# A two-layer graph kernel: biases spread by transposition, the last bank summed in PSUM in two pieces, and a load group moved one row tile later

## The chip, the core and the metric

The kernel runs on one core of a Trainium2 chip, in one launch. The metric is the device time in microseconds. Before the change its median is 930.77 us over three runs (930.59 to 931.49). The profile shown here is of one more execution of the same kernel, 930.15 us, whose instructions span 928.3 us.

## What is computed

There are 4096 nodes with 512 features each, a dense 4096 x 4096 adjacency matrix `adj`, and two layers, each with a residual. Cut to what matters:

```python
h = relu(layernorm(x))
# layer 0: attention within graphs of 128 nodes; the softmax is over the whole row
a = where(mask, (h @ Wq.T + bq) @ (h @ Wk.T + bk).T * scale, 0.0)
scores = (a + adj + adj) * where(mask, 1.0, -1e6)
x = x + (softmax(scores) * mask) @ (h @ Wv.T + bv)
# layer 1: graph attention with 8 heads of 64 features, over the edges adj > 0
h = relu(layernorm(x))
mx = einsum('nf,hfd->hnd', h, W)
logits = s_i[:, :, None] + t_j[:, None, :]
attn = softmax(where(adj > 0, logits, -inf))
x = x + concat_heads(attn @ mx)
```

In layer 1 the term `s_i` is the same for all neighbours of a row and cancels in the softmax. So a row's result is a masked sum of `exp(t_j) * mx_j` divided by the masked sum of `exp(t_j)`, and the aggregation is one product of the 0/1 mask with a table that holds both.

## The kernel before

**Tiling.** Rows go in 32 row tiles (`NT`) of 128 nodes. Features are four blocks of 128 (`KC`). TensorE multiplies a stationary operand of 128 columns, loaded anew for each matmul instruction, with a moving operand. A matmul of fp32 data is two instructions, one of float32r data is one, and a transposition of fp32 data is one.

**Start (`fold`, `spread_bias`).** The query and key weights are turned tile by tile (L205) and multiplied with each other (L242), so that layer 0 needs one product for its scores. The biases `bk` and `bq`, held with one feature to a partition, must be spread as rows over all partitions. For each block of 128 features, `spread_bias` multiplies a column broadcast to 128 x 128 with the identity (L187), and ScalarE copies the result to SBUF (L192). The same is done with the vector `u_col` (L231, copied at L235). ScalarE's order here is written by hand: the four copies of the key weights (L206), the two of the biases, the four of the query weights. TensorE's order here is the scheduler's.

**Layer 0.** It goes over pairs of row tiles, in an order written by hand for all engines. The adjacency matrix streams through SBUF once, 64 loads of 1 MB, and what layer 1 needs of it, a mask of one byte per edge, is written to DRAM. The queue of the sync engine (SP) issues these loads in program order, and each waits until its buffer is free and for what was issued ahead of it.

**Between the layers.** Layer 1's table is made for row tiles 8 to 31 by a loop over `i`. In step `i` the sync queue loads row `i + 12` (`load`, L775), VectorE and ScalarE normalise row `far = i + 10`, and VectorE turns it (`turn`). After each fourth row `store` writes the group of four to DRAM (L420), and `move` brings it back transposed as `hT4` (four loads, L428), which waits for that store to land. TensorE projects tile `i` (L271), ScalarE takes the exponential, VectorE multiplies (`weigh`, L280), and `split` makes the table `parts[i]` of two float32r parts, the rounded value and what is left of it[...]. When `far` is 33 the buffers of the rows are given up, and the mask words of the first row tile are loaded (`load_words`, L291).

**Layer 1's aggregation.** The table has 522 columns (512 of features, 8 of denominators, 2 spare), as `CB` = 3 banks of `CW1` = 174. A matmul of `product` (L322) takes one bank with both parts side by side, 348 columns, which lie side by side in PSUM:

```python
nc.tensor.matmul(
    pg[:, : 2 * CW1].rearrange("p (s w) -> p s w", s=2)[:, :, :n],
    at[:, j, :], part(j)[:, c, :, :n],
    start=(j == 0), stop=(j == NT - 1),
)
```

A row tile is 32 x 3 such matmuls. After them ScalarE copies the first part and VectorE adds the second. The last row tile goes bank by bank, in the order 2, 0, 1, so that most of its closing work lies beside matmuls. For each bank ScalarE copies the first part (L887), VectorE adds the second (L888), multiplies by the reciprocal of the denominators (`rb`, L905) and adds the row of layer 0 (L906), and the store is issued from ScalarE's queue (L907). Bank 2 comes first because it holds the denominators. A check of the fast path's conditions is folded into one number (`bad_i`, L900 to L903), and the branch on it at the end skips a general version.

Of the kernel before, what the change touches and what calls it, by code (L numbers as in the profile page):

```python
# [9 lines left out]
F32 = mybir.dt.float32  # L10
# [5 lines left out]
ALU = mybir.AluOpType  # L16
# [4 lines left out]
P = 128  # L21
N = 4096
D = 512
NT = N // P
# [5 lines left out]
BY = 4  # L30
# [6 lines left out]
CB = 3  # L37
CW1 = 174
# [6 lines left out]
AHEAD = 10  # L45
WARM = 10
LO = 8
# [6 lines left out]
def kernel(  # L54
# [22 lines left out]
    nc = tc.nc  # L77
# [13 lines left out]
    ident = const.tile([P, P], F32, name="ident")  # L91
# [82 lines left out]
    def fold(sb, tmp, work, ps_t, ps_p, loads, between):  # L174

        wkT_sb = load_weight(tmp, wkT, "wkT_sb", KC, tag="lo")
        nc.sync.dma_start(bk_sb, bk)
        nc.sync.dma_start(bq_sb, bq)  # L180
        wqT_sb = load_weight(tmp, wqT, "wqT_sb", KC, tag="lo")
        loads()

        def spread_bias(b):
            pp = ps_p.tile([P, D], F32, name="pp")
            for k in range(KC):
                nc.tensor.matmul(  # L187
                    pp[:, ts(k, P)], b[:, k : k + 1].to_broadcast([P, P]), ident,
                    start=True, stop=True,
                )  # L190
            row = work.tile([P, D], F32, name="b_row", tag="hn")
            nc.scalar.copy(row, pp)  # L192
            return row


        pt = ps_t.tile([P, KC, P], F32, name="pt")
        for _ in range(WARM):
            nc.tensor.transpose(pt[:, 0, :], ident, ident)
        nat = []
        for n, wT in enumerate((wkT_sb, wqT_sb)):  # L200
            w = tmp.tile([P, KC, D], F32, name=f"w{n}", tag="lo")
            for k in range(KC):
                pt = ps_t.tile([P, KC, P], F32, name="pt")
                for m in range(KC):
                    nc.tensor.transpose(pt[:, m, :], wT[:, k, ts(m, P)], ident)  # L205
                nc.scalar.copy(w[:, :, ts(k, P)], pt)  # L206
                if n == 0 and k == KC - 1:
                    rows = [spread_bias(b) for b in (bk_sb, bq_sb)]
            nat.append(w)
        wk, wq = nat  # L210
        m_sb = sb.tile([P, KC, D], F32, name="m_sb")
        c_sb = sb.tile([P, KC], F32, name="c_sb")
        u_col = sb.tile([P, KC], F32, name="u_col")
        u_sb = sb.tile([P, D], F32, name="u_sb")
        z_sb = sb.tile([P, 1], F32, name="z_sb")
        for dst, wT, row in ((u_col, wqT_sb, rows[0]), (c_sb, wkT_sb, rows[1])):
            for k in range(KC):
                wb = work.tile([P, D], BF16, name="wb", tag="hu", bufs=1)
                nc.vector.scalar_tensor_tensor(
                    wb, wT[:, k, :], SCALE, row, ALU.mult, ALU.mult, accum_out=dst[:, k : k + 1]  # L220
                )
        zk = sb.tile([P, KC], F32, name="zk")
        zp = sb.tile([P, 1], F32, name="zp")
        nc.vector.scalar_tensor_tensor(
            zk, bq_sb, SCALE, bk_sb, ALU.mult, ALU.mult, accum_out=zp
        )
        for m in range(KC):
            if m == 2:
                pp = ps_p.tile([P, D], F32, name="pp")
                for k in range(KC):  # L230
                    nc.tensor.matmul(  # L231
                        pp[:, ts(k, P)], u_col[:, k : k + 1].to_broadcast([P, P]), ident,
                        start=True, stop=True,
                    )
                nc.scalar.copy(u_sb, pp)  # L235
                pp = ps_p.tile([P, D], F32, name="pp")
                nc.tensor.matmul(pp[:, :1], zp.to_broadcast([P, P]), one, start=True, stop=True)
                nc.scalar.copy(z_sb, pp[:, :1])
            between(m, 0)
            pp = ps_p.tile([P, D], F32, name="pp")  # L240
            for k in range(KC):
                nc.tensor.matmul(  # L242
                    pp, wq[:, k, ts(m, P)], wk[:, k, :], start=(k == 0), stop=(k == KC - 1)
                )
            between(m, 1)
            nc.scalar.mul(m_sb[:, m, :], pp, SCALE)
        return m_sb, c_sb, u_sb, z_sb
# [138 lines left out]
    parts = []  # L386
    with ExitStack() as straight:
# [4 lines left out]
        with ExitStack() as prep:  # L392
# [71 lines left out]
            with (  # L464
# [160 lines left out]
                first = []  # L625
# [151 lines left out]
            with by_hand:  # L777
                ahead = LO + AHEAD + 5
                for i in range(LO + AHEAD, ahead):
                    load(i)  # L780
                move(LO // BY + 1)
                before = None
                low = lambda: None
                for i in range(LO, NT):
                    far = i + AHEAD
                    if far + 2 >= ahead:
                        load(far + 2)
                    if far % BY == 1 and LO + AHEAD < far <= NT + 1:
                        move(far // BY - 1)
                    if far == NT + 1:  # L790

                        begun.close()
                        sb3a = straight.enter_context(
                            tc.tile_pool(name="sb3a", bufs=1, reuse_waits="tile")
                        )
                        ata = sb3a.tile([P, NT, P], F32R, name="ata")
                        words = load_words(sb3a, 0)
                    if i == NT - 4:
                        at8 = turn_words(sb3a, words)
                    if i in (NT - 3, NT - 2):  # L800
                        half = (i - NT + 3) * NW // 2
                        widen(ata, at8, half, half + NW // 2)
                    low()
                    if far < NT:
                        of[far] = moments(rows[far])
                    if LO + AHEAD < far <= NT:
                        turn(far - 1, rows[far - 1], (keep, sb4)[(far - 1) // BY % 2])
                        if far % BY == 0:
                            store(far // BY - 1)
                    pm = project1(ps_p, hTs[i], w1x)  # L810
                    if before:
                        low = finish(*before, later=True)
                    if far < NT:
                        norm(rows[far], rows[far], of[far])
                    before = (weights(i, pm), pm, upper[i])
                    if far < NT:
                        nc.scalar.activation(rows[far], rows[far], AF.Relu)
                low()
                finish(*before)
# [55 lines left out]
        at = mask_of(i)  # L875
        ps_l = straight.enter_context(tc.tile_pool(name="ps_l3", bufs=2, space=PSUM))
        tot = sb3.tile([P, EW], F32, name="tot")
        rb = sb3.tile([P, EW], F32, name="tot")
        for c in (CB - 1, 0, 1):
            if c == 1:  # L880
                pg = ps_g.tile([P, CB, 512], F32, name="pg")[:, 0]
            else:
                pg = ps_l.tile([P, 512], F32, name="pl")
            for j in range(NT):
                product(pg, at, lambda j: parts[j], j, c, False)
            part = tot[:, ts(c, CW1)]
            nc.scalar.copy(part, pg[:, :CW1])  # L887
            nc.vector.tensor_tensor(part, part, pg[:, CW1 : 2 * CW1], ALU.add)  # L888
            if c == CB - 1:
                r = heads_rest(tot)  # L890
                nc.vector.tensor_scalar(held[:, 5:6], tot[:, ES : ES + 1], 0.0, None, ALU.is_gt)
                all_held = small.tile([P, 1], F32, name="all_held")
                nc.vector.tensor_reduce(all_held, held, AX.X, ALU.min)
                nc.vector.tensor_copy(
                    rb[:, :D].rearrange("p (h d) -> p h d", d=HD),
                    r[:, :, None].to_broadcast([P, H, HD]),
                )
            if c == 0:
                pt = ps_g.tile([P, CB, 512], F32, name="pg")[:, 0, :P]
                nc.tensor.transpose(pt[:1, :], all_held, ident)  # L900
                least = small.tile([1, 1], F32, name="least")
                nc.vector.tensor_reduce(least, pt[:1, :], AX.X, ALU.min)
                nc.vector.tensor_scalar(bad_i, least, 1.0, None, ALU.is_lt)  # L903
            here = slice(c * CW1, min((c + 1) * CW1, D))
            nc.vector.tensor_tensor(tot[:, here], tot[:, here], rb[:, here], ALU.mult)  # L905
            nc.vector.tensor_tensor(tot[:, here], tot[:, here], row[:, here], ALU.add)  # L906
            nc.scalar.dma_start(out[ts(i, P), here], tot[:, here])  # L907
    bad = nc.values_load(bad_i[0:1, 0:1], min_val=0, max_val=1)
# [294 lines left out]
```

## Time and profile before

| | |
|---|---|
| time, median of 3 | 930.77 us |
| span of the profiled execution | 928.3 us |
| TensorE's clock granted | 0.999 |
| aggregation, 31 row tiles (from the chain of waits) | 473.07 us, 2976 matmuls |
| its last row tile, banks 2 and 0 | 10.21 us, 64 matmuls |
| its last row tile, bank 1 | 5.16 us, 32 matmuls |
| two spread biases (L187) | 16 matmul instructions, 1.2 us and 1.2 us busy |
| spread `u_col` (L231) | 8 matmul instructions, 1.1 us busy |

The page gives each engine's busy time over the whole span. The chain of waits follows the end of the run back to what released each step. A line of a group names the line of the kernel, the engine, what is written from what, the shapes and the count, then busy time and the mean of one, then the idle time ahead of it and what ended that. PE stands for TensorE's matmuls and PEld for its weight loads, which can run beside them. DVE is VectorE, ACT is ScalarE, POOL is GpSimd, and SPq and ACTq are the queues of DMA issues.

### The profile page before, as it was taken

What the parts mean: (1) busy time and instruction counts of PE and PEld (TensorE: products, weight loads), DVE (VectorE), ACT (ScalarE), POOL (GpSimd) and SP (SyncE); (2) the same over time, 40 slices, a digit from 0 to 9 for tenths busy, and PEclk for the clock granted to TensorE, in tenths of its full rate; (3) what the DMA queues carried; (4) which work ended last, traced back from release to release, by engine and by line L of the source; (5) the groups of instructions that cost most, each with busy time, mean ns of one, the idle gap of its engine ahead of it and who ended that gap; (6) DMA issues with size and microseconds to landing.
All of it is one profiled execution on the core that took longest, in us unless ns stands there. A gap on an engine that the chain in (4) does not pass through costs nothing.

```text
span 928.3 us, 13021 instructions
## 1 busy us (share of the span) xinstructions
PE 919.4 (99%) x4933; PEld 803.4 (87%) x4933; DVE 474.3 (51%) x1016; ACT 261.1 (28%) x507; POOL 160.8 (17%) x344
## 2 busy tenths in 40 slices
PE   9999999999999999999999999999999999999997
PEld 6776676767767778889999999999999999999997
DVE  4577987677778776736272424232333323242412
ACT  5477667655566653321000000000000000000000
POOL 1112111132211225644010101010101010101010
PEclk9999999999999999999999999999999999999999
DMA  8999999999899766762212122222222131313111
GB/s 333 415 333 390 366 372 377 345 368 352 309 350 370 238 203 182 208 154 57 69 52 85 55 83 61 76 69 68 82 56 83 55 91 46 91 46 92 46 46 37
DMA packets 63941, 165.01 MB, mean 178 GB/s; under 512 B 7042, under 2 KB 23810, under 8 KB 54658
## 3 DMA queue, kind: packets, MB, share of 16 engines
q1 hardware_dynamic: 54370, 147.35, 47.4%
q10 hardware_dynamic: 9504, 16.78, 4.8%
q8 instruction: 40, 0.66, 0.3%
q14 instruction: 27, 0.22, 0.1%
HBM read 122.16 MB, written 41.94 MB: 177 GB/s over the span
## 4 chain that ended last, share of the span: by engine, by line
PE 90%; DMA 6%; DVE 1%; ACT 1%; POOL 1%; issue 0%; SPq 0%; DVEq 0%; ACTq 0%
PE pg L322 52%; PE pp L517 10%; PE pp L504 10%; PE pp L271 9%; PE pss L578 3%; PE pp L609 3%; DMA xg<-x 2%; PE pp L242 1%; DMA row<-x_d 1%; PE pt L135 1%; DMA x_d<-x 1%; PE pl L322 1%; DMA a<-adj 1%; DMA hT_d<-blocks 0%; DMA bk_sb<-bk 0%
## 5 line engine op out<-in xcount | busy, mean ns | idle before, releaser
L322 PE MATMUL pg<-part,ata 128*128 128x348 f32 (+1 forms) x1536 | 246.8, 321 | 0.0
L322 PEld LDWEIGHTS pg<-part,ata 128*128 128x128 f32 x1536 | 244.5, 188 | 0.1
L322 PE MATMUL pg<-part,atb 128*128 128x348 f32 x1472 | 236.8, 322 | 0.0
L322 PEld LDWEIGHTS pg<-part,atb 128*128 128x128 f32 x1472 | 234.6, 189 | 0.1
L336 ACT COPY tot<-pg 128x522 f32<-128x522 f32 x31 | 18.5, 597 | 454.0 <-PE pg L322 454.0
L547 ACT ACTIVATE junk<-a 128x2048 bf16<-128x2048 f32 (+15 forms) x92 | 124.5, 1353 | 1.3
L517 PE MATMUL pp<-wv,hT 128*128 128x512 f32 x256 | 114.9, 592 | 0.0
L308 DVE CAST atb<-at 128x4096 fp32r<-128x4096 fp8e4 x16 | 36.7, 2295 | 152.6 <-PE pg L322 152.6
L271 PE MATMUL pp<-w1x,hT 128*128 128x256 f32 (+1 forms) x512 | 114.1, 383 | 0.3 <-DVE e L280 0.3
L504 PE MATMUL pp<-hT,m_sb 128*128 128x256 f32 x512 | 113.2, 379 | 0.0
L271 PEld LDWEIGHTS pp<-w1x,hT 128*128 128x128 f32 x512 | 96.7, 190 | 16.2 <-issue 1.9
L308 DVE CAST ata<-at 128x4096 fp32r<-128x4096 fp8e4 (+1 forms) x17 | 36.9, 2168 | 140.5 <-PE pg L322 140.4
L504 PEld LDWEIGHTS pp<-hT,m_sb 128*128 128x128 f32 x512 | 96.2, 190 | 12.8 <-issue 0.5
L517 PEld LDWEIGHTS pp<-wv,hT 128*128 128x128 f32 x256 | 47.9, 190 | 54.3 <-issue 53.5
L144 DVE TENSOR_SCALAR a<-a 128x512 fp8e4<-128x512 f32 x256 | 90.4, 447 | 1.3 <-DMA a<-adj 1.3
L854 POOL COPY den_all<-tot 128x1 f32<-128x1 f32 x31 | 5.7, 184 | 365.9 <-DVE tot L337 365.9
L858 POOL TENSOR_TENSOR tot<-tot,row 128x512 f32<-128x512 f32 x31 | 39.9, 1287 | 61.9 <-DVE tot L342 59.9
L121 POOL TENSOR_SCALAR ve<-mv 128x1 f32<-128x1 f32 x64 | 15.1, 236 | 190.4 <-DVE mv L119 190.3
L255 POOL TENSOR_TENSOR part<-e,part 128x522 fp32r<-128x522 f32 x32 | 40.7, 1271 | 12.8 <-ACT part L252 12.8
L123 POOL TENSOR_TENSOR rstd<-ve,neghalf 128x1 f32<-128x1 f32 x64 | 41.1, 642 | 5.3
L299 DVE STREAM_TRANSPOSE at<-mw 128x1024 f32<-128x1024 f32 x32 | 39.6, 1237 | 0.0
L280 DVE TENSOR_TENSOR e<-pp,e 128x256 f32<-128x256 f32 x64 | 25.1, 411 | 27.0 <-PE pp L271 13.7
(114 smaller groups left out, 658.4 us busy)
## 6 DMA issues: line engine op xcount, KB each, us to landing
a<-adj SPq DMA_DIRECT2D x64, 1024.0 KB, 8.4
a_d<-a SPq DMA_DIRECT2D x32, 512.0 KB, 9.0
mw<-a_d SPq DMA_DIRECT2D x128, 128.0 KB, 3.9
row<-x_d SPq DMA_DIRECT2D x60, 256.0 KB, 3.7
xg<-x SPq DMA_DIRECT2D x16, 512.0 KB, 10.7
x_d<-x ACTq DMA_DIRECT2D x32, 256.0 KB, 7.3
hT_d<-blocks SPq DMA_DIRECT2D x8, 1024.0 KB, 4.8
hT<-hT_d SPq DMA_DIRECT2D x32, 256.0 KB, 6.2
```

The source lines that it names most:

```text
L123: nc.gpsimd.tensor_tensor(rstd, ve, neghalf, ALU.pow)
L144: nc.vector.tensor_scalar(a8v[:, u], av[:, u], 0.0, None, ALU.is_gt, saturate=False)
L255: nc.gpsimd.tensor_sub(dst[:, :, 1, :], e3, dst[:, :, 0, :].bitcast(F32))
L271: nc.tensor.matmul(pm[g][:, :n], hT[:, k, :], w1x[:, k, g * HW : g * HW + n], start=(k == 0), stop=(k == KC - 1),)
L299: nc.vector.transpose(at8.rearrange("p c n b -> p (c n b)").bitcast(F32).rearrange("p (c u n) -> p c u n", c=NW, n=B), mw.rearrange("p u ( ...
L308: nc.vector.tensor_copy(at[:, c0 * BY : c1 * BY].rearrange("p (c b) q -> p c b q", b=BY), at8[:, c0:c1].rearrange("p c q b -> p c b q"),)
L322: nc.tensor.matmul(pg[:, : 2 * CW1].rearrange("p (s w) -> p s w", s=2)[:, :, :n], at[:, j, :], part(j)[:, c, :, :n], start=(j == 0), stop= ...
L504: nc.tensor.matmul(pp[:, : G * P], m_sb[:, k, ts(m, P)], hT[:, k, :], start=(k == 0), stop=(k == KC - 1),)
L517: nc.tensor.matmul(pp, hT[:, k, ts(t, P)], wv[:, k, :], start=(k == 0), stop=(k == KC - 1))
L547: nc.scalar.activation(junk[:, c0:c1], a[:, c0:c1], AF.Exp, scale=2.0 * NEG, accum_out=sums[:, n : n + 1],)
L578: nc.tensor.matmul(pss[:, t, :], gT[:, k, ts(t, P)], hT[:, k, ts(t, P)], start=(k == 0), stop=(k == KC - 1),)
L858: nc.gpsimd.tensor_add(num, num, row)
```

## The change

There are three edits. The first spreads the two biases and `u_col` with transpositions of the broadcast column in place of matmuls with the identity. The second moves `move`, for the groups that it handles in the loop between the layers, from the step after the store to one step later, so that one more row load stands ahead of it in the sync queue. The third treats the last bank of the last row tile in two pieces of 88 and 86 columns. Both parts of each row tile are added up in the same PSUM columns by two matmuls, so that no copy and no addition is left after them, and the second piece alone is left to be closed at the end.

```diff
         def spread_bias(b):
             pp = ps_p.tile([P, D], F32, name="pp")
             for k in range(KC):
-                nc.tensor.matmul(
-                    pp[:, ts(k, P)], b[:, k : k + 1].to_broadcast([P, P]), ident,
-                    start=True, stop=True,
-                )
+                nc.tensor.transpose(pp[:, ts(k, P)], b[:, k : k + 1].to_broadcast([P, P]), ident)
...
-                    nc.tensor.matmul(
-                        pp[:, ts(k, P)], u_col[:, k : k + 1].to_broadcast([P, P]), ident,
-                        start=True, stop=True,
+                    nc.tensor.transpose(
+                        pp[:, ts(k, P)], u_col[:, k : k + 1].to_broadcast([P, P]), ident
                     )
...
-                    if far % BY == 1 and LO + AHEAD < far <= NT + 1:
+                    if far % BY == 2 and LO + AHEAD < far <= NT + 2:
                         move(far // BY - 1)
...
-        for c in (CB - 1, 0, 1):
+        CW2 = CW1 // 2 + 1
+        for c, c0, w in ((CB - 1, 0, CW1), (0, 0, CW1), (1, 0, CW2), (1, CW2, CW1 - CW2)):
+            first = c * CW1 + c0
+            here = slice(first, min(first + w, D))
             if c == 1:
-                pg = ps_g.tile([P, CB, 512], F32, name="pg")[:, 0]
+                pg = ps_g.tile([P, CB, 512], F32, name="pg")[:, 0, :w]
+                for j in range(NT):
+                    for part in range(2):
+                        nc.tensor.matmul(
+                            pg, at[:, j, :], parts[j][:, c, part, c0 : c0 + w],
+                            start=(j + part == 0), stop=(j == NT - 1 and part == 1),
+                        )
+                nc.vector.tensor_tensor(tot[:, here], pg, rb[:, here], ALU.mult)
             else:
                 pg = ps_l.tile([P, 512], F32, name="pl")
-            for j in range(NT):
-                product(pg, at, lambda j: parts[j], j, c, False)
-            part = tot[:, ts(c, CW1)]
-            nc.scalar.copy(part, pg[:, :CW1])
-            nc.vector.tensor_tensor(part, part, pg[:, CW1 : 2 * CW1], ALU.add)
+                for j in range(NT):
+                    product(pg, at, lambda j: parts[j], j, c, False)
+                part = tot[:, ts(c, CW1)]
+                nc.scalar.copy(part, pg[:, :CW1])
+                nc.vector.tensor_tensor(part, part, pg[:, CW1 : 2 * CW1], ALU.add)
...
-            here = slice(c * CW1, min((c + 1) * CW1, D))
-            nc.vector.tensor_tensor(tot[:, here], tot[:, here], rb[:, here], ALU.mult)
+            if c != 1:
+                nc.vector.tensor_tensor(tot[:, here], tot[:, here], rb[:, here], ALU.mult)
             nc.vector.tensor_tensor(tot[:, here], tot[:, here], row[:, here], ALU.add)
```

## The prediction, made before the changed kernel was run

> **What bounds the kernel now.** I read the page first, then TensorE's waits, the chain of waits, the weight loads by shape, and three stretches in order of time. On the page TensorE is busy for all but 9 us:
>
> ```profile
> PE 919.4 (99%) x4933; PEld 803.4 (87%) x4933; DVE 474.3 (51%) x1016; ACT 261.1 (28%) x507; POOL 160.8 (17%) x344
> ```
>
> There is one weight load (PEld) for each matmul instruction. The list of TensorE's waits (us in total, times, longest) shows how little there is to win in the middle:
>
> ```profile
> PE pp L609 <- DVE e L280: 0.8, 1, 0.8
> ...
> PE pp L271 <- DVE e L280: 0.3, 1, 0.3
> PE pt L205 <- ACT w L206: 0.2, 1, 0.2
> ```
>
> The rest of the 9 us lies before the first data and after the last matmul. So removed matmul time counts, a removed wait counts 0.3 us, and work that is added to TensorE is added to the end. The end of the chain of waits (start, us, what):
>
> ```profile
> 917.57 5.16 PE pg L322 x32
> 922.75 0.31 ACT tot L887
> 923.09 0.35 DVE tot L888
> 923.46 0.35 DVE tot L905
> 923.84 0.34 DVE tot L906
> ```
>
> The last bank takes 32 matmuls in 5.16 us, 0.161 us each for 348 columns, and then four small operations in a row from 922.75 to 924.18 before the last store is issued.
>
> What decides this case is how fast narrow matmuls can follow one another, so I look at weight loads by shape (count, busy us, mean ns of one):
>
> ```profile
> L322 PEld LDWEIGHTS pg<-part,atb 128*128 128x128 f32 x1472 | 234.6, 189 | 0.1
> ...
> L205 PEld LDWEIGHTS pt<-ident,wqT_sb 128*128 128x128 f32 x16 | 1.8, 141 | 0.4 <-ACT w L206 0.4
> ...
> L900 PEld LDWEIGHTS pg<-ident,all_held 128*1 128x1 f32 x1 | 0.1, 82 | 0.0
> ```
>
> A load of one column takes 82 ns, a full one in the aggregation 189: 107 ns for 127 more columns. The loads of transpositions take 141, so 59 more. Whether a load bounds the pace shows where matmuls are tiny, in order of time (start, us):
>
> ```profile
> 18.93 0.30 PEld L237 LDWEIGHTS pp<-one,zp 128*128 128x128 f32 x2
> 19.03 0.28 PE L237 MATMUL pp<-one,zp 128*128 128x1 f32 x2
> ...
> 19.15 0.30 PEld L242 LDWEIGHTS pp<-w,w 128*128 128x128 f32 x2
> ```
>
> Matmuls of one column each, yet the loads start at 18.93 and 19.15 with one between: **0.11 us a matmul, whatever its width.** At 348 columns the 0.161 us of streaming hides that; at 88 it can't.
>
> [...] Loads of L322 have the length of the FP32 ones (189 against 190 at L271)[...]
>
> **The change part by part.**
>
> *Last bank.* Removed: 32 matmuls, 5.16 us. Added: 2 pieces x 32 tiles x 2 parts = 128 matmuls of 88 or 86 columns. Each brings its own load, also where two in a row have the same weights: before, three in a row (one per bank) share `at[:, j]`, and the counts are still 4933 and 4933. By columns one would stream in 88 x 0.161/348 = 0.041 us; the load needs 0.11. No float32r matmul under 344 columns is in the trace, so I bound it. [...] Above: what a column costs in an ordinary fp32 matmul of 128 columns, two instructions of 0.112 (16 of L578 in 1.79 us), so 0.224/128 x 88 = 0.154. I take L237's 0.111: 128 x 0.111 = 14.2 us, +9.0; the last matmul drains some 0.1 sooner (322 ns for 348 columns, 169 for one, so about 210). Net **+8.9** (13.7 us and +8.4 below, 19.7 us and +14.4 above). Nothing else is on TensorE's queue behind it, and the end waits for it: all of it is on the path.
>
> *What follows the last matmul.* Before: 922.72 (end of the last matmul) to 924.21 (issue of the store), 1.49 us. After: one product out of PSUM and one addition, 86 columns each, [...] plus three hand-overs of 0.03: 0.60. **-0.9.** The first piece's product, addition and store lie beside the second piece's 7 us, and cost nothing. The second piece takes the other ps_g buffer, whose last reader (L902) is done by 917.9: no wait.
>
> *Biases by transposition.* An fp32 matmul is two instructions (x8 for four at L187), a transposition one (x16 for sixteen at L205). So 24 instructions of 0.111 become 12 of 0.109: 2.66 - 1.31 = 1.35 us off TensorE. Of the 0.9 from the two biases little arrives: L205's last four transpositions wait for ScalarE's copies already now (the 0.2 us above), and ScalarE's row of copies begins with the one at 8.67, whose four transpositions now follow 10 instructions (10 x 0.111) and then follow 8 (8 x 0.109), and 0.05 sooner by the quicker first load: 0.29 sooner. The 0.45 of u_col arrives in full, since u_col is ready at 16.3 and used at 18.1. Sum 0.74. But the next stage leans on the DMA, which is full (us, PE, PEld, DVE, ACT, POOL, clock, DMA share, GB/s):
>
> ```profile
> 40.00:60.00 20.00, 20.00 (x91) 14.14 (x90) 13.03 (x35) 12.53 (x25) 2.46 (x7) 1.00 0.89 335
> 60.00:80.00 20.00, 20.00 (x95) 14.30 (x94) 14.67 (x40) 13.35 (x26) 3.26 (x9) 1.00 1.02 390
> ```
>
> At 187 TensorE waits 0.8 us for `e`, whose VectorE sat behind an x load that landed late. If transfers alone set that moment, TensorE only waits 0.74 longer; the gap at 40 to 60 says buffers still have a word there, so part passes. **-0.5**, from 0 to -0.75.
>
> *The group moved later.* Between the layers the sync queue holds the hT loads of `move`, which wait for the store's landing, ahead of row loads. VectorE then waits for a row, and TensorE for VectorE:
>
> ```profile
> 386.40 0.69 DVE L117 BATCH_NORM_STATS2 stats<-row 128x6 f32<-128x512 f32 x1 [2.91 <-DMA row<-x_d]
> ...
> 388.36 45.83 PE L271 MATMUL pp<-w1x,hT 128*128 128x264 f32 x208 [0.29 <-DVE e L280]
> ```
>
> One more row load goes ahead of `move`: that row was issued at 380.30 and may now go at 374, landing before 383.5, where VectorE wanted it. hT is still loaded four tiles (14 us) ahead of use, against 6.2 us to land. **-0.3**, or 0 if the next row takes its place. The order now lets the mask words of row tile 1 be turned (1.23 us on VectorE) ahead of a product L280; its PSUM buffer is wanted over 3 us later, so nothing.
>
> Sum: +8.9 - 0.9 - 0.5 - 0.3 = **+7.2, 938.0 us.**
>
> **Rivals.**
> 1. *Narrow float32r matmuls stream no quicker than fp32* (0.154): +14.4 - 1.7 = +12.7, 943.5 us. For it: no narrow one is in the trace. Against: 344 and 348 columns run at about a quarter of fp32's cost per column (0.46 against 1.75 ns).
> 2. *The second load of the same weights is free, or loads go as quickly as those of transpositions* (59 ns): 7.0 to 7.6 us, about +2 - 0.1 - 1.7, 931 us, no change. Against: 189 against 141 ns, and equal counts.
> 3. *Loads don't bound at all*: 128 x 0.041 = 5.2 us, no loss, and with all 1.35 of the biases -0.9 - 0.3 - 1.35 = -2.5, 928.3 us, **faster**. Against: L237's 0.11.
>
> **How the numbers follow.** Forecast 0.62, rival 1 0.26, rival 2 0.07, rival 3 0.05. The forecast spans 937.2 (+8.4 - 0.9 - 0.35 - 0.75) to 939.0 (0.1125 a matmul, +9.1 - 0.9, no gain elsewhere); rival 1 spans 942.8 (0.150) to 945.2 (0.160). The range 936.8 to 945.0 holds both, 0.87. Slower 0.88, within 0.2% (1.9 us) 0.07, faster 0.05.
>
> **What would show it.** The chain's last TensorE piece grows from 5.16 to about 14.2 us, with 0.11 between matmuls; 0.15 is rival 1, 0.06 rival 2, 0.04 rival 3. From the last matmul's end to the store's issue: 0.6 us. L271 without a wait on L280. The wait before L609 at 187: 0.8 us if the biases' gain passes, up to 1.5 if the DMA keeps it. Wrong would be a time under 936, which needs narrow matmuls quicker than their loads.

## The result, and the profile after

The changed kernel takes **945.92 us** (median of six runs, 945.04 to 948.83) against 930.62 (929.95 to 931.49) before: 1.0168 times the time, with an interval of 1.0153 to 1.0183. The forecast of slower was right, but the size was not: +15.3 us against +7.2, just outside the range of 936.8 to 945.0. Line numbers from here on are those of the changed kernel, whose matmuls of `product` stand at L318 and whose new narrow ones at L884.

The end of its chain of waits (start, us, what):

```profile
904.88 10.21 PE pl L318 x64
915.09 0.11 PE pg L907
915.20 23.55 PE pg L884 x128
...
938.78 0.26 DVE tot L888
...
939.06 0.25 DVE tot L913
```

The span grew by 15.0 us (928.3 to 943.3), and the two chains say where. The last row tile is reached at 904.88 instead of 907.26, -2.38. The last bank takes 23.55 us instead of 5.16, +18.39. What follows it takes 4.55 us (938.75 to 943.3) instead of 5.57 (922.73 to 928.3), -1.02. The sum is +14.99, so the whole loss lies in the last bank, and it is more than the other two edits and the shorter close give back.

23.55 us over 128 matmuls is 0.184 us each, above every price in the prediction. But a mean hides what happened. The narrow matmuls alone, in three stretches (us, PE busy, PEld busy, TensorE's clock, DMA share, GB/s; a count in brackets includes instructions that lie across an edge of the stretch):

```profile
915.20:918.90 3.70, 3.70 (x36) 3.70 (x35) 1.00 0.12 31
918.95:922.00 3.05, 3.05 (x17) 3.05 (x16) 0.52 0.02 5
922.00:938.70 16.70, 16.70 (x79) 16.58 (x78) 0.50 0.01 4
```

For 3.7 us they come at 0.11 us each, as forecast. **Then the clock column falls to 0.50**, and the same instructions come at 0.213. The groups of their weight loads say it too, in the first stretch and in a later one (count, busy us, mean ns of one, idle before):

```profile
L884 PEld LDWEIGHTS pg<-part,atb 128*128 128x128 f32 x35 | 4.0, 192 | 0.0
...
L884 PEld LDWEIGHTS pg<-part,atb 128*128 128x128 f32 x89 | 19.1, 333 | 0.0
```

On the page the engine looks as busy as ever; only the clock's row shows a change, in its last digit:

```profile
PE   8999999999999999999999999999999999999998
...
PEclk9999999999999999999999999999999999999995
```

PE's 9 means that instructions followed one another without a pause. It doesn't say that the array was at work: 88 columns are streamed in some 0.041 us, an estimate from the wide matmuls (88/348 of 0.161), while the matmuls come 0.111 us apart and weight loads are busy for all of it (3.70 of 3.70 us). In the trace's record of the clock the fall is at 919.07, and the record stays at 0.50 for the 26.2 us that are left of it. The first narrow matmul starts at 914.96, 4.1 us earlier (the chain counts it from 915.20, when the work ahead of it has drained). Such times after the first narrow matmul are counted from its own start from here on.

### The profile page after: what moved, and what is told of

Same layout as the page of the kernel before. It is cut to its first block, busy times and chain, and to the rows that moved or that the text cites. A ratio compares the mean times of both kernels' runs of the same rounds, so it can differ in the third digit from the quotient of the medians.

```text
span 943.3 us, 13191 instructions
## 1 busy us (share of the span) xinstructions
PE 935.5 (99%) x5017; PEld 820.0 (87%) x5017; DVE 475.2 (50%) x1017; ACT 261.1 (28%) x506; POOL 162.3 (17%) x344
## 4 chain that ended last, share of the span: by engine, by line
PE 99%; DMA 0%; ACT 0%; SPq 0%; DVE 0%; issue 0%
PE pg L318 50%; PE pp L267 12%; PE pp L500 12%; PE pp L513 12%; PE pss L574 3%; PE pp L605 3%; PE pg L884 2%; PE pt L135 1%; PE pp L238 1%; PE pl L318 1%; DMA bk_sb<-bk 0%; PE pss L597 0%; SPq L152 0%; PE pt L202 0%; PE pp L187 0%; ACT w L203 0%
## 5 line engine op out<-in xcount | busy, mean ns | idle before, releaser
L318 PE MATMUL pg<-part,ata 128*128 128x348 f32 (+1 forms) x1536 | 246.8, 321 | 0.0
L318 PEld LDWEIGHTS pg<-part,ata 128*128 128x128 f32 x1536 | 244.4, 188 | 0.1
L318 PE MATMUL pg<-part,atb 128*128 128x348 f32 (+1 forms) x1440 | 231.5, 321 | 0.0
L318 PEld LDWEIGHTS pg<-part,atb 128*128 128x128 f32 x1440 | 229.5, 188 | 0.0
```

The lines of the kernel that those rows point to most:

```text
L318: nc.tensor.matmul(pg[:, : 2 * CW1].rearrange("p (s w) -> p s w", s=2)[:, :, :n], at[:, j, :], part(j)[:, c, :, :n], start=(j == 0), stop= ...
```

## The experiments

**The theory,** which the runs below are to test: TensorE's clock is lowered when the array streams too little over a stretch of a few microseconds (4.1 in the changed kernel), even if its queue never pauses. Matmuls of 88 columns, held to 0.111 us by their weight loads, stream too little, by the estimate above 0.37 of the time. **Rivals:** narrow float32r matmuls are slow in themselves (the prediction's rival 1); the clock falls because the run is ending; weight loads without a pause lower the clock, whatever is streamed.

What the expectations call a window of 3.4 us is a step in the records of the clock: it is full for 914.77 us in the changed kernel and in e4 (the last bank's edit alone), 918.19 in e1 (the other two edits) and 921.60 before, which is 268, 269 and 270 times 3.413 (in e1 and before, the fall comes after the last matmul).

### The parts of the change, one at a time

Three kernels take one or two of the three edits, with the rest as before. The fourth is the last bank's edit alone. e1 has the first two:

```diff
-                nc.tensor.matmul(
-                    pp[:, ts(k, P)], b[:, k : k + 1].to_broadcast([P, P]), ident,
-                    start=True, stop=True,
-                )
+                nc.tensor.transpose(pp[:, ts(k, P)], b[:, k : k + 1].to_broadcast([P, P]), ident)
...
-                    if far % BY == 1 and LO + AHEAD < far <= NT + 1:
+                    if far % BY == 2 and LO + AHEAD < far <= NT + 2:
```

e2 has the first hunk (with that of `u_col`), e3 the second, and e4 only the hunk of the last bank.

> Biases by transposition and the group moved later, last bank as before. The changed kernel's trace reached the last row tile's bank 2 at 904.88 us instead of 907.26, 2.4 us sooner, so the closing bank alone is the loss. This theory expects 930.6 - 2.4 = 928.2 us. Rival: part of the 2.4 us is chance of the transfers in one execution (the 1.0 us at 187); then 929.2 us. If the loss were spread elsewhere than in the last bank, it would stay above 931 us.

> Biases by transposition alone. Theory: TensorE reaches layer 0 0.65 us sooner, and the loads behind it follow, so the wait at 187 us disappears too (1.0 us): 930.6 - 1.7 = 928.9 us. Rival (as the prediction had it): the full DMA keeps the gain, the wait at 187 grows from 0.8 to 1.5 us, and the time is 930.3 us or more.

> The group moved later alone. Theory: both hitches of the loop between the layers go (0.14 us at 373, 0.53 us at 388, start to start): 930.6 - 0.67 = 929.95 us, and the wait at 187 stays. Rival: the wait at 187 is gone here too, so it was not the biases' doing: 928.9 us.

> The last bank in two pieces alone. Clock theory: matmuls of 88 columns follow at 0.111 us, TensorE's clock halves about 4 us after they begin, from then on 0.213: 36 x 0.111 + 92 x 0.213 = 23.6 us for 128, against 5.2, and 1.0 us less after it: 930.6 + 18.4 - 1.0 = 948 us, with a scatter of up to 3 us from where the halving falls. Rival, narrow matmuls are slow in themselves: the same pace from the first to the last, 0.18 each, and no scatter. Rival, the loads alone: 938.7 us.

| kernel | median us (runs) | ratio to before, interval |
|---|---|---|
| before | 930.98 (47) | |
| e1, biases and group | 929.40 (18) | 0.9985, 0.9978 to 0.9993 |
| e2, biases | 929.45 (22) | 0.9980, 0.9971 to 0.9989 |
| e3, group | 930.38 (14) | 0.9992, 0.9984 to 1.0001 |
| e4, last bank | 947.84 (5) | 1.0175, 1.0158 to 1.0193 |

The last bank's edit alone costs what the clock theory said (948), a little more than the whole change. The halving is in its trace as well, at 921.95, 3.5 us after the first narrow matmul there, and its last bank takes 24.13 us:

```profile
918.72 24.13 PE pg L888 x128
```

The scatter (946.07 to 949.0) fits too, but proves little, as the kernel before scatters as widely in many runs. By the medians the parts add up: +16.9 with the last bank alone and -1.6 with the other two edits make the +15.3 of the whole.

The other two edits together gain 1.4 us by their interval's middle (0.7 to 2.0). So the forecast of 2.4 less missed and its rival of 1.4 was close: the 2.4 us were read off single traces, and that of the changed kernel is the fastest of its six runs. The biases alone gain 1.5 us by the medians, near the 1.7 of the theory and not the 0.3 or less of the rival. The group alone gains 0.6, as forecast, but by its interval (-0.1 to 1.5) this can't be told from no change. The mechanism forecast for the biases did not show, though. TensorE's wait for `e` at about 187 us, 0.8 us before and none in e1 and the changed kernel, is 1.5 with the biases alone, where one more wait of 0.9 stands, and 1.3 and 1.8 in the traces of e3 and e4, whose start is untouched. The lines of e2, traced in its second slowest run of 22:

```profile
PE pp L605 <- DVE e L276: 1.5, 1, 1.5
PE pp L500 <- ACT hT L136: 0.9, 1, 0.9
```

Among before, e3 and e4, with the same start, this wait spreads over 1.0 us, so one trace can't say what an edit does to it. The likely cause is when transfers land; no run separates that. What doesn't vary is the group: with it, the projections gain 0.66 us over the loop between the layers in e1, in e3 and in the changed kernel alike. In e2, without the group, 0.48 of it went as well, in a trace where TensorE came to that loop 1.4 us later; in e4, also without it and 1.2 us later, 0.02 went. The runs don't say why e2's went. **e1 beats both kernels**; e2 can't be told from it.

### Narrow matmuls that stream more

```diff
-        for c, c0, w in ((CB - 1, 0, CW1), (0, 0, CW1), (1, 0, CW2), (1, CW2, CW1 - CW2)):
+        for c, c0, w in ((CB - 1, 0, CW1), (0, 0, CW1), (1, 0, CW1)):
```

> The changed kernel with its last bank in one piece: 64 matmuls of 174 columns, both parts summed in PSUM. [...] 174 columns stream for 0.081 (half of 0.161), so the array works some 0.7 of the time, against a third with 88 columns. Clock theory (the clock halves when the array streams for too little of a 3.4 us window): if 0.7 is enough, 64 x 0.111 = 7.1 us, 1.9 more than before, 0.7 less after it, about 930.6 us with the other two edits. If the loads' pace and not the array's share halves the clock: about 31 x 0.111 + 33 x 0.213 = 10.5 us, 934 us.

Measured: 930.74 us over 20 runs, 0.9998 of the kernel before (0.9989 to 1.0006). The last bank in its chain, and the clock in its stretches (us, PE busy, clock, DMA share, GB/s):

```profile
917.58 7.13 PE pg L884 x64
```

```profile
917.60:924.70 7.10, 7.10 (x64) 1.00 0.11 25
```

64 matmuls of 174 columns come at 0.111 us, the same as with 88, and the clock holds to the end. So the weight load sets the pace of either (0.11 us also between the loads of the one-column matmuls before), and the pace of the loads doesn't by itself lower the clock. This also says what summing in PSUM is worth: 1.97 us more on TensorE, 0.7 less after it (0.78 us from its last matmul to the store's issue instead of 1.49), so a loss of some 1.3 us that the other two edits make good.

### Wide matmuls after the narrow ones

```diff
-        for c, c0, w in ((CB - 1, 0, CW1), (0, 0, CW1), (1, 0, CW2), (1, CW2, CW1 - CW2)):
+        for c, c0, w in ((CB - 1, 0, CW1), (1, 0, CW2), (1, CW2, CW1 - CW2), (0, 0, CW1)):
```

> The changed kernel with the last row tile's banks in the order 2, 1 (two narrow pieces), 0, so that 32 matmuls of 348 columns follow the narrow ones. Clock theory: the narrow ones take 21 to 24.4 us as before; the wide ones begin at twice their time, 0.32 us each, and go back to 0.161 at the end of a window of 3.4 us. Bank 0 then takes 5.2 + 1.7 to 3.4, some 7 to 8.6 us. Rival, the clock falls because the run is ending: the narrow ones take 14.3 us. Rival, narrow matmuls are slow in themselves: bank 0 takes 5.2.

Measured: 949.19 us in one run. Its chain, then its stretches (us, PE busy, clock, DMA share, GB/s):

```profile
910.54 22.51 PE pg L884 x128
933.05 6.57 PE pl L318 x32
```

```profile
910.60:915.40 4.80, 4.80 (x45) 1.00 0.33 114
915.60:932.80 17.20, 17.20 (x83) 0.50 0.01 4
933.10:936.00 2.90, 2.90 (x11) 0.50 0.06 15
936.20:939.60 3.40, 3.40 (x23) 1.00 0.00 0
```

The narrow matmuls lower the clock here too, with 32 wide ones still to come, so the end of the run is not the cause. The wide ones inherit the half clock: the first ten start 0.29 us apart (0.32 was expected), and then they are back at 0.16. Bank 0 takes 6.57 us instead of 5.16, a little under the 7 expected, as the clock was back at 1.00 some 3 us after its start. That wide ones suffer, and that the first narrow ones come at 0.11, rules out that narrow ones are slow in themselves.

### The same narrow matmuls among wide ones

```diff
+        for c, c0, w in ((CB - 1, 0, CW2), (0, CW2, CW1 - CW2)):
...
+            for j in range(NT):
+                for half in range(2):
+                    nc.tensor.matmul(
+                        two[:, 0, :w], at[:, j, :], parts[j][:, 1, half, c0 : c0 + w],
+                        start=(j + half == 0), stop=(j == NT - 1 and half == 1),
+                    )
+                product(wide, at, lambda j: parts[j], j, c, False)
```

> The same 128 narrow matmuls, but two of them ahead of each of the 64 wide ones of banks 2 and 0. Loads still come back to back, three in 0.33 us, but the array streams for (2 x 0.04 + 0.16) of it, 0.7. Clock theory by the array's share: full clock to the end, 64 x 0.333 = 21.3 us for the row tile where the changed kernel takes 10.2 + 23.6. Rival, the loads' pace or the narrow matmuls as such lower the clock: over 30 us, and half the clock in the record.

Measured: 939.20 us in one run. The stretches of its last row tile:

```profile
906.20:918.20 12.00, 12.00 (x96) 1.00 0.16 45
918.30:930.30 12.00, 12.00 (x97) 1.00 0.04 11
```

The 128 narrow instructions of the changed kernel are all here, each with its load, and the clock stays at 1.00. The row tile takes some 24.5 us instead of 33.9. Three matmuls take 0.382 us, not the 0.333 expected, so by the estimate above the array streams (2 x 0.041 + 0.161)/0.382 = 0.64 of the time. The loads start 0.168, 0.110 and 0.111 us apart, the long step behind the wide matmul. An estimate that fits these times has only one load run ahead of the present matmul: the wide matmul hides one load, and each narrow one waits for the next: 0.161 + 2 x 0.111 = 0.383. No run tests it further.

### Where the limit lies

The changed kernel with other widths of its two pieces:

```diff
-        CW2 = CW1 // 2 + 1
+        CW2 = 130
```

> The changed kernel with pieces of 130 and 44 columns: 64 matmuls at a load's pace with the array at work for about 0.06 of 0.111 us, 0.54, then 64 with 0.18. Clock theory: whether the clock holds through the first piece (7.1 us, at least one whole window) puts the limit above or below 0.54; in the second piece it falls at the latest by the end of its first whole window, 3.4 to 6.8 us after its start. A clock that held through both would speak against it.

> The changed kernel with pieces of 110 and 64 columns. With 130 columns the clock held through a whole window, with 88 it fell at the end of the first. 110 columns stream for some 0.051 of 0.111 us, 0.46. Clock theory: a fall at the end of the first whole window inside the first piece (7.1 us) puts the limit above 0.46, a fall only in the second piece (0.27) below it.

> The changed kernel with pieces of 98 and 76 columns: 98 columns stream for 0.045 of 0.111 us, 0.41, between 88 (0.37, fell) and 110 (0.46). Clock theory: as for 110 columns, the place of the fall says on which side of the limit it lies; it can't hold here if it fell with 110. In any case it falls by the end of the first whole window of the second piece (0.31).

One run each: 940.64, 941.03 and 943.22 us. In stretches, e8 with 130 and 44 columns (the second piece begins at 923.8):

```profile
920.00:923.30 3.30, 3.30 (x32) 1.00 0.04 5
923.40:926.70 3.30, 3.30 (x32) 1.00 0.07 20
926.80:934.80 8.00, 8.00 (x39) 0.50 0.01 2
```

e9 with 110 and 64 (the second begins at 923.7):

```profile
920.00:923.40 3.40, 3.40 (x33) 1.00 0.03 6
923.50:926.80 3.30, 3.30 (x32) 1.00 0.06 17
926.90:934.70 7.80, 7.80 (x38) 0.50 0.01 2
```

e10 with 98 and 76, still in its first piece when the clock falls:

```profile
918.70:922.00 3.30, 3.30 (x32) 1.00 0.06 6
922.10:923.30 1.20, 1.20 (x8) 0.50 0.00 0
```

With 130 and with 110 columns per 0.111 us the first piece keeps the clock, and it falls in the second. With 98 it falls in the first, 6.4 us after its start. All three have the same 128 matmuls at the same pace of loads, so **what is streamed decides**: 98 columns per 0.111 us are too few, 110 are enough. Taking 348 columns in 0.161 us as full, that is between 0.41 and 0.46 of it. This bracket rests on one run at each width and on a clock held for 7.2 us, so it is an estimate for this kernel.

## Why the prediction was right and wrong

**The last bank, the step that failed.** The working said "128 x 0.111 = 14.2 us". Its price was right: the first 37 come at 0.1116 us. What failed is that one price was applied to all 128. The other 91 come at 0.2133, so that 37 x 0.1116 + 91 x 0.2133 = 23.5 us, and the term is +18.4, not +8.9. The working bounded what a load and what a column costs (its low figure of 13.7 us is 128 times the 107 ns by which a full load is longer than one of one column), and put a change of the clock at nothing without a word; the page before shows nines in every slice of its clock row. It had the figure that mattered, 0.041 us of streaming in 0.111, and read it only as a pace. A sign stood in the trace before, too. Its first transpositions start 0.213 us apart up to 5.2 us, those from 6.2 us on 0.109 apart, and the record of the clock begins only at 5.56 us; the row counts what lies ahead of that as full. In the changed kernel the step from 0.213 to 0.110 lies between 4.14 and 4.33 us, and its record begins at 4.30. 0.213 is also the pace of the narrow matmuls after the fall. The loads of these transpositions take 226 ns, against 141 for those of L205 that the prediction shows:

```profile
L198 PEld LDWEIGHTS pt<-ident 128*128 128x128 f32 x10 | 2.0, 226 | 1.5 <-POOL ident masks.py:199 1.5
```

**Rival 1** would have been nearer by its time, 943.5 us, and is wrong by its cause: at its price the 174 columns of e5 would take 0.305 us (0.224/128 x 174) and they take 0.111, and e6 has slow wide ones. Rivals 2 and 3 fall by the 0.1116.

**What follows the last matmul, right.** Its own 0.60 us from the last matmul's end to the store's issue was measured as 0.60 (938.74 to 939.34), with 0.25 for each of its two operations. The trace before gives 0.25 for 86 columns as well, by an estimate from 0.34 at 174 (its L905) and 0.69 at 512 (its L342). The whole close shrank by 1.02 against 0.9 said.

**The group moved later, right in mechanism and too small.** Said -0.3, measured -0.66. The row that VectorE had waited 2.91 us for now goes at 369.45 and lands at 374.78, ahead of its use. The next row takes its place, as the prediction feared, but VectorE waits little for it, and TensorE not at all:

```profile
384.78 0.69 DVE L117 BATCH_NORM_STATS2 stats<-row 128x6 f32<-128x512 f32 x1 [0.62 <-DMA row<-x_d]
```

The term was mis-sized because 0.29 us of idle was read off the group. From start to start the matmul at 388.36 came 0.665 us after the one ahead of it, where 0.216 is usual, and its successor lost 0.07 more: 0.52. Another 0.14 went at 373.8, where no idle is shown. Idle is counted from a matmul's modelled end, and the end of one of these, 0.216 us apart, lies 0.38 after its start; a wait has to outlast that before it shows at all (0.665 less 0.38 leaves the 0.29).

**The biases, right at the start and open after it.** The first product of layer 0's stage was reached 0.64 us sooner against 0.74 said, and the missing 0.1 is `bk`, which landed that much later in this execution. From the first bias instruction to that product it is 19.44 us in the changed kernel (6.92 to 26.36), 19.43 in e1 and 19.44 in e2, against 20.18 before (6.82 to 27.00), so 0.74 sooner. In e3 and e4, with the old start, it is 20.14 and 20.53. The wait at 187 (0.8, or up to 1.5, was forecast) is gone in the changed kernel and 1.5 in e2, and reaches 1.8 where the start is untouched. The runs don't settle how much of the gain passes the full DMA (share 0.92 and 1.02 at 40 to 60 and 60 to 80 us in the changed kernel) in a given execution. By its interval the edit gains 1.0 to 2.7 us, over the 0.5 said, and both edits together 0.7 to 2.0, where 0.8 was said.

## What to carry to other kernels

A float32r matmul with its own weights took 0.111 us at every width tried at full clock (44 to 174 columns), so a sum moved into PSUM by halving the width of a matmul of 348 columns (0.161) adds time on TensorE, 1.97 us over 32 of them in e5. Before a stage is built of load-bound matmuls, work out what share of the time the array streams: by the estimate above the clock held at 0.46 of full rate over 7.2 us (e9), and at 0.41 it halved after 6.4 (e10). The wide work behind it began at the half clock too, for about 3 us in e6. In a profile, a row of nines for PE is no proof of a busy array; read the clock's row beside it, and the distance between like instructions, which pointed to a low clock at the start of the trace before (0.213 us against 0.109), where the row didn't.

## What the runs showed of the hardware that was not expected

- The clock halves under an unbroken queue of matmuls (88 columns per 0.111 us) and comes back about 3 us after wide ones follow (e6). Each change falls on a grid of 3.413 us (full, half and full again last 907.95, 20.48 and 6.83 us in e6: 266, 6 and 2 times that). In four runs the fall comes at the end of the first step of that grid that holds nothing but matmuls of 98 columns or fewer: 3.5 (e4), 4.1 (changed kernel), 5.2 (e6) and 6.4 us (e10) after the first of them, between one step and two.
- A load of weights slows with the clock, 192 to 333 ns each, and the pace from 0.1116 to 0.2133 us. The 0.382 us for three matmuls in e7 fit an estimate with one load ahead of the running matmul (0.383).
- Three programs with the same start (before, e3, e4) waited 0.8, 1.3 and 1.8 us at the same place of layer 0 in their traced executions.
